# Max over neighbours by table lookup: groups of 7 columns become pairs of groups of 6

## The chip, the cores and the metric

The kernel runs on one core of one Trainium2 chip. A core has five engines with queues of their own, each in order: TensorE (PE, with its weight loads shown apart as PEld), VectorE (DVE), ScalarE (ACT), GpSimd (POOL) and SyncE (SP, which only issues transfers here). They meet through semaphores. TensorE writes to PSUM, 8 banks of 512 fp32 columns on 128 partitions; VectorE and ScalarE read it from there. The metric is the device time of one execution in microseconds, median over runs.

## The reference, cut to what matters

Four graph layers run over 16 graphs of 1024 nodes with 128 features, each followed by a residual addition and a layer norm: an attention (layer 0), an edge layer with a maximum (layer 1), a sum aggregation with a small MLP (layer 2), and three aggregations over a thinned adjacency (layer 3). The change is in layer 1:

```python
p = jnp.einsum('bnd,do->bno', x, W1 - W2)
q = jnp.einsum('bnd,do->bno', x, W2)
pre = p[:, :, None, :] + q[:, None, :, :] + b
h = jax.nn.relu(pre) * adj[..., None]
return jnp.max(h, axis=2)
```

As p[i] and b don't depend on the neighbour j, this is relu(p[i] + b + max of q[j] over the neighbours j of i), with zero for a node without neighbours.

Layer 3 thins the adjacency first ("dilation"), row by row in order: a row's removals take effect on later rows.

## The kernel before

**The maximum as a lookup.** The 1024 columns of a graph are cut into NG = 147 groups of GS = 7. For each group and feature, a table holds the maximum of q over each of the 128 subsets of the group (`tables_of`, L454 and L458: 7 doublings on VectorE for TG = 12 groups at a time). Which subset a node's neighbours form is found by one matmul: `lit` has +1 and −1 by the bits of the subset, and relu(count + 1 − size) is one at the right subset and zero elsewhere. That is `count`: a matmul `pm` (L688) and the ScalarE activation `hot` (L689), for each half of 512 nodes. The table is turned by a transpose (`table`, L700) so that subsets lie on partitions, and split into a high part in fp32r (L702, ScalarE) and the rest (`low_part`, L708, VectorE), for three groups at a time. `look_up` (L714) multiplies both parts with `hot` into `pg`, a PSUM tile of 128 features by 1024 nodes, of which there are two. VectorE then takes the running maximum `best` (L756).

**The slots.** `slot(s)` writes the instructions of one group, in the order in which each engine's queue gets them; there are 16 × 147 slots. It first lets other work advance, then writes for each half a count (of the group two slots ahead) and a lookup, then the table of a later group, then the maximum. The other work consists of generators ("streams") that yield what they need next with `ask`: engine, an estimated cost, whether they take or give back the one shared PSUM bank, what must have happened, a delay in slots. `advance` takes a step where the room of its engine (`ROOM`, refilled in every slot) allows. The streams are `scores` and `attend` (layer 0 of the next graph, with q and p of layer 1), `rest` (the end of layer 1 of the previous graph, and layer 2), and `tables_of`.

**The dilation** runs beside this, in 32 stripes of 32 rows. It yields how many slots later its next step comes. In a stripe, VectorE makes the counts (`low`, `rest`, L551 and L553), GpSimd goes through 31 rows (L566 to L576), the result `hit` goes to memory and back by SyncE's queue as `hit_p`, and VectorE goes on with `hit_T` (L587), ranks (L613, with ScalarE at L616) and `gone` (L619). GpSimd also issues, in its own queue, the loads of `E` (L482), `AT` (L647) and `An` (L638), and does the layer norms' rows. `An`, the adjacency of a graph, is read first by ScalarE's `off` (L313).

Where a graph's slots end, `rest` adds p to `best` (L380) and takes relu on ScalarE.

Of the kernel before, what the change touches and what calls it, by code (L numbers as in the profile page):

```python
# [42 lines left out]
GS = 7  # L43
CH = 126
GC = CH // GS
NG = -(-N // GS)
# [11 lines left out]
def subset_tables():  # L58

    s = np.arange(P)  # L60
    lit = np.zeros((CH, GC, P), np.float32)
    for j in range(CH):
        lit[j, j // GS] = np.where((s >> (j % GS)) & 1, 1.0, -1.0)
    size = sum((s >> k) & 1 for k in range(GS))
    return lit, (1.0 - size).astype(np.float32).reshape(P, 1)
# [3 lines left out]
def tile_graph_layers(ctx: ExitStack, tc, a, out):  # L69
# [30 lines left out]
    lit = consts.tile([CH, GC, P], F8, name="lit")  # L100
# [126 lines left out]
    def layers_012():  # L227
# [17 lines left out]
        def ask(engine, cost, take=False, give=False, same=False, delay=1, after=None, third=False, urgent=False):  # L245
            return engine, cost, take, give or urgent and None, 0 if same else delay, after, third
# [19 lines left out]
        def columns_of(dst, src, first=1):  # L266
            for h in range(2):
                yield ask("PE", 0.44, take=True, delay=1 if h else first)
                p = shared("ptr")
                for t in range(4):  # L270
                    nc.tensor.transpose(p[:, t * P:(t + 1) * P], src[:, 4 * h + t, :], ident)
                yield ask("A", 0.59, give=True, same=True)
                nc.scalar.copy(dst[:, halves[h]], p)

        def product_of(lhsT, rhs, dst, func, bias, delay=1):
            for h, s in enumerate(halves):
                yield ask("PE", 0.86, take=True, delay=1 if h else delay)
                p = shared("pp")
                nc.tensor.matmul(p, lhsT, rhs[:, s], start=True, stop=True)
                yield ask("A", 0.6, give=True, same=True)  # L280
                if bias is None:
                    nc.scalar.copy(dst[:, s], p)  # L282
                else:
                    nc.scalar.activation(dst[:, s], p, func, bias=bias)

        def scores(b):
# [51 lines left out]
            q = w4.tile([P, NG * GS], F32, name="q", bufs=2)  # L338
# [3 lines left out]
            happened["q", b] = now  # L342
            p = ps[b] = w4.tile([P, N], F32, name="p", bufs=2)
# [33 lines left out]
        def rest(b):  # L377
            best, p = bests.pop(b), ps.pop(b)
            yield ask("V", 1.2, after=("rest", b - 1) if b else None)
            nc.vector.tensor_add(best, best, p)  # L380
            yield ask("A", 1.06)
            nc.scalar.activation(best, best, AF.Relu)
            y = w4.tile([P, T, D], F32, name="y1", tag="y")
            for h in range(2):
                yield ask("PE", 0.44, take=True)
                pt = shared("ph")
                for t in range(4):
                    nc.tensor.transpose(pt[:, t * P:(t + 1) * P],
                                        best[:, (4 * h + t) * P:(4 * h + t + 1) * P], ident)
                yield ask("V", 0.66, give=True, same=True)  # L390
                nc.vector.tensor_add(y[:, 4 * h:4 * h + 4, :], X[b][:, 4 * h:4 * h + 4, :],
                                     pt.rearrange("p (t d) -> p t d", d=D))
            yield from norm(X[b], y)
# [49 lines left out]
        def tables_of(b):  # L443

            if b:
                yield ask("V", 0, urgent=True, after=("tables", b - 1))
            for g0 in range(0, NG, TG):
                n_g = min(TG, NG - g0)
                yield ask("V", 0.01, same=True, urgent=True, after=("q", b))
                made.append((b, g0))  # L450
                yield ask("V", 0.1, same=True, urgent=True, after=("used", *made[-3]) if len(made) > 2 else None)
                qg = qs[b].rearrange("o (g s) -> o g s", s=GS)
                sub = subs[b, g0] = w2.tile([P, TG, P], F32, name="sub", bufs=2)
                nc.vector.memset(sub[:, :n_g, 0:1], LOWEST)  # L454
                for k in range(GS):
                    n = 1 << k
                    yield ask("V", 0.06 + n * n_g / 960, same=(n < 8), urgent=True)
                    nc.vector.tensor_max(sub[:, :n_g, n:2 * n], sub[:, :n_g, 0:n],  # L458
                                         qg[:, g0:g0 + n_g, k:k + 1].to_broadcast([P, n_g, n]))
                happened["sub", b, g0] = now  # L460
            happened["tables", b] = now
# [10 lines left out]
        def dilation():  # L472
# [62 lines left out]
            for k in range(K):  # L535
# [21 lines left out]
                yield 1, 0.5  # L557
                gp = nc.gpsimd
                for n in range(R - 1):
# [17 lines left out]
                    yield 1.35, 0.06  # L577
# [7 lines left out]
                yield B * NG / K - 60.85, 0  # L585
# [6 lines left out]
                yield 1, 0.5  # L592
# [16 lines left out]
                yield 1, 0.5  # L609
                for q in range(Q):  # L610
                    rank = dil.tile([P, N], F32, name="rank", bufs=2)
                    for h, s in enumerate(halves):
                        nc.vector.tensor_tensor_scan(rank[:, s], E[:, q, s], E[:, q, s], rank[:, 511:512] if h else 0.0,  # L613
                                                     op0=ALU.add, op1=ALU.max)
                        yield 0.75, 1.2
                    nc.scalar.activation(rank, rank, AF.Abs, bias=centre[:, q:q + 1], scale=scale[:, q:q + 1])  # L616
                    yield 0.75, 0
# [4 lines left out]
                    yield 0.75, 1.3  # L622
# [5 lines left out]
                    yield 0.75, 0.8  # L628
# [26 lines left out]
        ROOM = {"PE": 0.6, "A": 0.6, "V": 1.4, "Pool": 9.0}  # L655
# [6 lines left out]
        def advance(engines):  # L662
            nonlocal bank_free
            for stream in list(streams):
                while True:
# [11 lines left out]
                    if give:  # L677
                        bank_free = now + 1
                    pending[stream] = [next(stream, None), now]

        def count(s, h):

            b, g = divmod(s, NG)
            c, r = divmod(g, GC)
# [6 lines left out]
        def table(s):  # L691

            b, g = divmod(s, NG)
            g0 = g - g % TG
            assert ("sub", b, g0) in happened, (s, [(x.__name__, pending[x]) for x in streams], room)
            pt = tables_bank("pt")[:, :3 * P]
            if g + 3 - g0 == min(TG, NG - g0):
                happened["used", b, g0] = now
            for k in range(3):
                nc.tensor.transpose(pt[:, k * P:(k + 1) * P], subs[b, g0][:, g - g0 + k, :], ident)  # L700
            high = w2.tile([P, 3 * P], F32R, name="high", bufs=2)
# [3 lines left out]
        def low_part(s):  # L705
            pt, high = tables[s]
            low = w2.tile([P, 3 * P], F32R, name="low", bufs=2)
# [3 lines left out]
        def look_up(s, h, pg):  # L711
            at = s % 3
            for k, part in enumerate(tables[s - at]):
                nc.tensor.matmul(pg[:, halves[h]], part[:, at * P:(at + 1) * P], hots[s][:, halves[h]],  # L714
                                 start=(k == 0), stop=(k == 1))

        def slot(s, last):

            nonlocal now, due
# [3 lines left out]
            b, g = divmod(s, NG)  # L723
            if s >= 0 and g == 0:
                bests[b] = w4.tile([P, N], F32, name="best", bufs=2)
# [7 lines left out]
            if s >= 0 and g % GC == 0:  # L733
                load_columns(b * (T + 1) + g // GC + 2)
            if (s + 1) % 3 == 0 and s + 1 < last:
# [4 lines left out]
            pg = psum.tile([P, N], F32, tag="wide", name="pg", bufs=2) if s >= 0 else None  # L740
            for h in range(2):
                if ahead is not None:
                    count(ahead, h)
                if s >= 0:
                    look_up(s, h, pg)
            if ahead is not None and ahead % 3 == 0:
                table(ahead)
            if s >= 0:
                while due <= s and s % 3 != 1:
                    after, cost = next(dilate, (B * NG, 0))  # L750
                    due += after
                    room["V"] -= cost
                if g == 0:
                    nc.vector.tensor_copy(bests[b], pg)
                else:
                    nc.vector.tensor_max(bests[b], bests[b], pg)  # L756
                hots.pop(s)

        dilate = dilation()
        due = 0.0  # L760
# [16 lines left out]
        with tc.manual_schedule(engines={mybir.EngineType.PE, mybir.EngineType.Activation, mybir.EngineType.DVE,  # L777
                                         mybir.EngineType.Pool}):
            planned = True
            for s in range(-2, B * NG):  # L780
                slot(s, B * NG)
# [313 lines left out]
```

## Time and profile before

| | us |
|---|---|
| runs: median of 3 (lowest to highest) | 7475.35 (7465.12 to 7479.03) |
| the profiled execution's own time | 7480.7 |
| its span in the profile | 7479.0 |
| busy: TensorE / weight loads | 6163.2 / 3818.6 |
| busy: VectorE | 5429.3 |
| busy: ScalarE | 4756.7 |
| busy: GpSimd | 3706.4 |
| `hot` L689, 4704 of 690 ns | 3119.1 |
| `best` L756, 2336 of 1214 ns | 2837.1 |

A group's line gives engine, operation, output and inputs with their shapes, the count, then busy time in us and the mean of one in ns, then how long the engine idled just ahead of these instructions and what ended most of that. Busy TensorE rows overlap each other: each reaches from its start to the modelled end of its last column, and the next starts before that. So a matmul's mean is its latency, not the pitch at which matmuls follow each other.

### The profile page before, as it was taken

The numbers are of one execution on the slowest core, as the hardware profiler recorded it, in microseconds if no ns is written. First come the engines' busy times: TensorE is split into PE (matmuls) and PEld (weight loads), VectorE is DVE, ScalarE is ACT, GpSimd is POOL, SyncE is SP. The second block draws the span as 40 slices with busy tenths as digits, with TensorE's granted clock in tenths as the row PEclk, the third lists the DMA queues.
The fourth block names the chain that finished last, engine by engine and source line by source line (L and its number), as shares of the span: only waits on it lengthen the run. The fifth ranks groups of instructions, "written<-read, shape, count | busy, mean of one in ns | idle before, by whom it ended". The sixth has DMA issues, their size and how long they took to land.

```text
span 7479.0 us, 89183 instructions
## 1 busy us (share of the span) xinstructions
PE 6163.2 (82%) x27882; PEld 3818.6 (51%) x27882; DVE 5429.3 (73%) x8907; ACT 4756.7 (64%) x7513; POOL 3706.4 (50%) x11637
## 2 busy tenths in 40 slices
PE   6878888888888878787978888787879767888996
PEld 4545555555554545454545455554545434555653
DVE  3878888878878878787878788787878764444453
ACT  4767777667776767676767676666667652333751
POOL 3455656565656555555555655555556531110116
PEclk8989999999999999999999999999989988888998
DMA  4121212121212121212121211111111025665544
GB/s 34 18 24 18 30 18 30 18 29 18 30 18 29 18 29 18 29 18 29 18 29 18 29 19 23 24 23 24 23 24 20 13 28 99 113 116 108 189 158 152
DMA packets 493633, 319.32 MB, mean 43 GB/s; under 512 B 315876, under 2 KB 444774, under 8 KB 489060
## 3 DMA queue, kind: packets, MB, share of 16 engines
q0 software_dynamic: 104880, 84.33, 13.0%
q1 hardware_dynamic: 383600, 228.10, 10.7%
q8 instruction: 219, 3.59, 0.2%
q10 hardware_dynamic: 4676, 1.19, 0.1%
q14 instruction: 258, 2.11, 0.1%
HBM read 414.24 MB, written 118.16 MB: 71 GB/s over the span
## 4 chain that ended last, share of the span: by engine, by line
PE 29%; DVE 15%; POOL 7%; ACT 5%; issue 3%; DMA 2%; ACTq 0%; SPq 0%; DVEq 0%; POOLq 0%
PE pg L714 9%; DVE best L756 6%; PE pagg L875 5%; PE pm L688 4%; DVE rank L613 2%; ACT hot L689 1%; DMA An<-in_adj_dram 1%; PE pa L411 1%; PE pav L368 1%; DVE sub L458 1%; PE psc L322 1%; PE pt L700 1%; PE po L889 1%; ACT rank L616 1%; DVE gone L619 1%
## 5 line engine op out<-in xcount | busy, mean ns | idle before, releaser
L689 ACT ACTIVATE hot<-pm,one_less 128x512 fp32r<-128x512 f32 x4704 | 3119.1, 690 | 1086.9 <-PE pm L688 1067.3
L756 DVE TENSOR_TENSOR best<-best,pg 128x1024 f32<-128x1024 f32 x2336 | 2837.1, 1214 | 776.7 <-PE pg L714 745.6
L714 PE MATMUL pg<-hot,high 128*128 128x512 f32 x4704 | 2825.2, 601 | 327.1 <-DVE best L756 324.8
L688 PE MATMUL pm<-AT,lit 126*128 126x512 fp8e4 x4704 | 1882.2, 400 | 165.6 <-ACT hot L689 163.8
L714 PE MATMUL pg<-hot,low 128*128 128x512 f32 x4704 | 1912.8, 407 | 0.0
L714 PEld LDWEIGHTS pg<-hot,high 128*128 128x128 f32 x4704 | 962.3, 205 | 772.5 <-DVE best L756 538.1
L688 PEld LDWEIGHTS <-lit 126*128 126x128 fp8e4 x4704 | 470.0, 100 | 1168.7 <-issue 1124.9
L714 PEld LDWEIGHTS pg<-hot,low 128*128 128x128 f32 x4704 | 935.2, 199 | 152.2 <-DVE low L708 21.0
L482 POOL DMA_DIRECT2D E<-in_adj_dram x128 | 70.3, 558 | 1621.3 <-DVE gone L619 1297.2
L458 DVE TENSOR_TENSOR sub<-sub,q 128x12 f32<-128x12 f32 (+7 forms) x1456 | 541.8, 372 | 32.7 <-ACT q L282 11.0
L566 POOL TENSOR_SCALAR sc<-low_counts,half_mask,rest 16x1 f32<-16x1 f32 x992 | 359.9, 363 | 252.5 <-DVE rest L553 156.1
L571 POOL TENSOR_SCALAR sc<-sc 16x1 f32<-16x1 f32 x992 | 412.9, 416 | 104.5
L708 DVE TENSOR_TENSOR low<-pt,high 128x384 fp32r<-128x384 f32 x784 | 431.6, 551 | 34.5 <-ACT high L702 34.3
L702 ACT CAST high<-pt 128x384 fp32r<-128x384 f32 x784 | 378.7, 483 | 102.4 <-PE pt L700 49.0
L700 PE MATMUL pt<-ident,sub 128*128 128x128 f32 x2352 | 406.2, 284 | 0.0
L568 POOL TENSOR_SCALAR sc<-sc 16x1 f32<-16x1 f32 x992 | 335.1, 338 | 107.1
L700 PEld LDWEIGHTS pt<-ident,sub 128*128 128x128 f32 x2352 | 322.6, 147 | 120.3 <-issue 14.3
L573 POOL TENSOR_SCALAR hit<-V,sc 16x31 bf16<-16x31 bf16 (+30 forms) x992 | 363.5, 366 | 0.0
L905 POOL TENSOR_TENSOR length<-length,mhalf 128x8 f32<-128x8 f32 x48 | 79.0, 1645 | 570.4 <-DVE length L904 570.4
L574 POOL TENSOR_SCALAR last_rank<-V,sc 16x31 f32<-16x31 bf16 (+30 forms) x992 | 356.4, 359 | 0.0
L322 PE MATMUL psc<-kT,qT 128*128 128x512 f32 x512 | 285.0, 640 | 67.2 <-DVE e L325 38.0
L862 ACT CAST m<-near 128x1024 fp32r<-128x1024 fp8e4 x256 | 253.8, 1044 | 119.3 <-PE pagg L875 54.2
(241 smaller groups left out, 9120.6 us busy)
## 6 DMA issues: line engine op xcount, KB each, us to landing
removed<-gone SPq DMA_DIRECT2D x128, 256.0 KB
An<-in_adj_dram POOLq DMA_DIRECT2D x16, 1024.0 KB, 13.5
E<-in_adj_dram POOLq DMA_DIRECT2D x128, 128.0 KB, 5.8
gone_all<-removed POOLq DMA_DIRECT2D x64, 256.0 KB, 12.4
near<-in_adjT_dram POOLq DMA_DIRECT2D x16, 1024.0 KB, 17.5
h<-x SPq DMA_DIRECT2D x32, 512.0 KB
kept<-near SPq DMA_DIRECT2D x16, 1024.0 KB
share<-share SPq DMA_DIRECT2D x32, 512.0 KB
```

Of the source, the lines that this page charges most:

```text
L458: nc.vector.tensor_max(sub[:, :n_g, n:2 * n], sub[:, :n_g, 0:n], qg[:, g0:g0 + n_g, k:k + 1].to_broadcast([P, n_g, n]))
L566: gp.tensor_scalar(half, mine, half_mask[:, m], rest[:, n:n + 1], op0=ALU.mult, op1=ALU.add)
L571: gp.tensor_scalar(to, at, sf, none, op0=ALU.subtract, op1=ALU.subtract)
L573: gp.tensor_scalar(hit[:, n, n + 1:], V[:, n, n + 1:], at, None, op0=ALU.is_equal)
L688: nc.tensor.matmul(pm, lit[:, r, :], AT[b * (T + 1) + c][:, halves[h]], start=True, stop=True)
L689: nc.scalar.activation(hots[s][:, halves[h]], pm, AF.Relu, bias=one_less)
L700: nc.tensor.transpose(pt[:, k * P:(k + 1) * P], subs[b, g0][:, g - g0 + k, :], ident)
L702: nc.scalar.copy(high, pt)
L708: nc.vector.tensor_sub(low, pt, high.bitcast(F32))
L714: nc.tensor.matmul(pg[:, halves[h]], part[:, at * P:(at + 1) * P], hots[s][:, halves[h]], start=(k == 0), stop=(k == 1))
L756: nc.vector.tensor_max(bests[b], bests[b], pg)
L875: nc.tensor.matmul(pa[:, s], piece[:, c, :], m[c][:, s], start=(c == 0 and k == 0), stop=(c == T - 1 and k == 1))
```

## The change

Columns are now taken in pairs of groups: PS = 12 columns, two groups of GS = 6, NP = 86 pairs in a graph, so 16 × 86 = 1376 slots. A group of 6 has 64 subsets, and the two groups of a pair share the 128 partitions: subsets of the first on 0 to 63, of the second on 64 to 127. One count matmul of 120 columns (ten pairs; before 126) serves both groups. `look_up` multiplies rows 0 to 63 into one bank and rows 64 to 127 into another, so `pg` is now 128 features by two groups by 512 nodes, one tile for each half of nodes. `best` has both groups apart, with a maximum for each half of nodes; `finish`, at a graph's end, takes the maximum over the two and adds p, which `rest` did before. Tables are turned and split for two pairs at a time. In the slot, both counts come first, then all lookups; TensorE's streams may advance once more behind the lookups, and those of the other engines between the two maxima, so delays are in half slots. The dilation's steps are spread anew over a stripe of 43 slots, and its step that needs the tables' bank is held to odd slots.

```diff
-GS = 7
-CH = 126
-GC = CH // GS
-NG = -(-N // GS)
+GS = 6
+PS = 2 * GS
+PC = 10
+CH = PC * PS
+NP = -(-N // PS)
...
-    lit = np.zeros((CH, GC, P), np.float32)
+    lit = np.zeros((CH, PC, P), np.float32)
     for j in range(CH):
-        lit[j, j // GS] = np.where((s >> (j % GS)) & 1, 1.0, -1.0)
+        a, k = divmod(j % PS, GS)
+        lit[j, j // PS, a * half:(a + 1) * half] = np.where((s >> k) & 1, 1.0, -1.0)
...
+            if b > 1:
+                yield ask("A", 0, same=True, after=("y1", b - 2))
             p = ps[b] = w4.tile([P, N], F32, name="p", bufs=2)
...
         def rest(b):
-            best, p = bests.pop(b), ps.pop(b)
-            yield ask("V", 1.2, after=("rest", b - 1) if b else None)
-            nc.vector.tensor_add(best, best, p)
-            yield ask("A", 1.06)
+            best = ps.pop(b)
+            yield ask("A", 1.06, after=("rest", b - 1) if b else None)
             nc.scalar.activation(best, best, AF.Relu)
...
-                sub = subs[b, g0] = w2.tile([P, TG, P], F32, name="sub", bufs=2)
+                subs[b, g0] = w2.tile([P, TG, P], F32, name="sub", bufs=2)
+                sub = subs[b, g0].rearrange("o t (a s) -> o (t a) s", a=2)
...
-                    yield 1.35, 0.06
+                    yield 0.95, 0.06, False
...
-                yield B * NG / K - 60.85, 0
+                yield B * NP / K - 37.75, 0, False
...
-                        yield 0.75, 1.2
+                        yield 0.34, 1.2, False
...
-        ROOM = {"PE": 0.6, "A": 0.6, "V": 1.4, "Pool": 9.0}
+        ROOM = {"PE": 1.2, "A": 0.8, "V": 1.4, "Pool": 9.0}
...
         def look_up(s, h, pg):
-            at = s % 3
+
+            at = s % 2
             for k, part in enumerate(tables[s - at]):
-                nc.tensor.matmul(pg[:, halves[h]], part[:, at * P:(at + 1) * P], hots[s][:, halves[h]],
-                                 start=(k == 0), stop=(k == 1))
+                for a in range(2):
+                    rows = slice(64 * a, 64 * a + 64)
+                    nc.tensor.matmul(pg[:, a], part[rows, at * P:(at + 1) * P], hots[s][rows, halves[h]],
+                                     start=(k == 0), stop=(k == 1))
+
+        def finish(b):
+
+            if b:
+                best = bests.pop(b - 1)
+                nc.vector.tensor_max(best[:, 0], best[:, 0], best[:, 1])
+                nc.vector.tensor_add(ps[b - 1], best[:, 0], ps[b - 1])
+            if b < B:
+                bests[b] = w4.tile([P, 2, N], F32, name="best")
...
-            pg = psum.tile([P, N], F32, tag="wide", name="pg", bufs=2) if s >= 0 else None
-            for h in range(2):
-                if ahead is not None:
+            if ahead is not None:
+                for h in range(2):
                     count(ahead, h)
-                if s >= 0:
-                    look_up(s, h, pg)
-            if ahead is not None and ahead % 3 == 0:
-                table(ahead)
+            pgs = []
             if s >= 0:
-                while due <= s and s % 3 != 1:
-                    after, cost = next(dilate, (B * NG, 0))
+                for h in range(2):
+                    pgs.append(psum.tile([P, 2, 512], F32, tag="wide", name="pg", bufs=2))
+                    look_up(s, h, pgs[h])
+                hots.pop(s)
+            now = s + 0.5
+            advance(("PE",))
+            if s >= 0:
+                while due <= s and (s % 2 or not wants_bank):
+                    after, cost, wants_bank = next(dilate, (B * NP, 0, False))
                     due += after
                     room["V"] -= cost
+            if ahead is not None and ahead % 2 == 0:
+                table(ahead)
+            for h, pg in enumerate(pgs):
+                if h:
+                    advance(("A", "V", "Pool"))
+                own = bests[b][:, :, halves[h]]
                 if g == 0:
-                    nc.vector.tensor_copy(bests[b], pg)
+                    nc.vector.tensor_copy(own, pg)
                 else:
-                    nc.vector.tensor_max(bests[b], bests[b], pg)
-                hots.pop(s)
+                    nc.vector.tensor_max(own, own, pg)
```

## The prediction

> **What bounds the kernel now.** I read the busy table by stretches first, then the groups by line, then who waited for whom, then the timeline. Three stretches: before the first maximum, the planned stretch of layers 0 to 2 (from the first `best` to the last, read off the groups and their first and last start), and layer 3. Columns: length, then each engine's busy time, clock, DMA share, GB/s.
>
> ```profile
> 0.00:141.50 141.50, 78.67 (x331) 51.23 (x332) 32.75 (x127) 45.86 (x71) 32.24 (x65) 0.86 0.64 44
> 141.50:6151.40 6009.90, 5013.30 (x22697) 3104.34 (x22695) 4816.35 (x7716) 4195.89 (x6808) 3412.51 (x11072) 0.94 0.17 23
> 6151.40:7479.00 1327.60, 1071.26 (x4856) 663.02 (x4856) 580.17 (x1067) 514.93 (x634) 261.70 (x500) 0.89 0.53 132
> ```
>
> Only the middle stretch is changed. It has 2352 slots (16 graphs of 147 groups), so a slot lasts 6009.9/2352 = 2.555 us. VectorE works 2.05 us of it, ScalarE 1.78, and no engine is full. Groups of the page (busy, mean ns, idle before):
>
> ```profile
> L689 ACT ACTIVATE hot<-pm,one_less 128x512 fp32r<-128x512 f32 x4704 | 3119.1, 690 | 1086.9 <-PE pm L688 1067.3
> L756 DVE TENSOR_TENSOR best<-best,pg 128x1024 f32<-128x1024 f32 x2336 | 2837.1, 1214 | 776.7 <-PE pg L714 745.6
> L714 PEld LDWEIGHTS pg<-hot,high 128*128 128x128 f32 x4704 | 962.3, 205 | 772.5 <-DVE best L756 538.1
> L458 DVE TENSOR_TENSOR sub<-sub,q 128x12 f32<-128x12 f32 (+7 forms) x1456 | 541.8, 372 | 32.7 <-ACT q L282 11.0
> L708 DVE TENSOR_TENSOR low<-pt,high 128x384 fp32r<-128x384 f32 x784 | 431.6, 551 | 34.5 <-ACT high L702 34.3
> ```
>
> TensorE's busy rows overlap each other, so I take its pitch from the timeline: one count, one high and one low lookup go from 2001.10 to 2001.78, 0.227 us each.
>
> ```profile
> 2001.10 0.38 PE L688 MATMUL pm<-AT,lit 126*128 126x512 fp8e4 x1
> 2001.12 0.58 PE L714 MATMUL pg<-hot,high 128*128 128x512 f32 x1
> 2001.55 0.40 PE L714 MATMUL pg<-hot,low 128*128 128x512 f32 x1
> 2001.78 0.39 PE L688 MATMUL pm<-AT,lit 126*128 126x512 fp8e4 x1
> ```
>
> A slot holds six of these (1.36 us), on average one table transpose (0.11) and 0.45 of other layers' matmuls: 1.92 us. VectorE and TensorE are thus nearly equal, and each waits for the other whenever their loads differ locally. VectorE's waits in the stretch (total us, times, longest):
>
> ```profile
> DVE best L756 <- PE pg L714: 745.6, 896, 30.6
> DVE e L325 <- PE psc L323: 166.4, 37, 27.7
> DVE hit_T L587 <- DMA hit_p<-hit: 69.5, 5, 33.3
> DVE gone L619 <- ACT rank L616: 62.7, 66, 2.9
> ```
>
> With L708 (31.8), L551 (25.7) and crumbs (91) that is 6009.9 − 4816.4 = 1193.5 us idle.
>
> **What the skill says.** "TensorE: Matmul & The Clock Gate", Part 3 (Packing small matmuls): matmuls whose rows lie in different row groups run at once; four of 32 rows measured 3.07 times faster. The trace of before has no such pair, so nothing here confirms it. Same page, LDWEIGHTS: a weight load costs by its columns, not its rows. The trace has 205 and 199 ns for 128 fp32r columns, against 0.227 us a matmul: hidden now, but halving the rows may not halve it. "TensorEngine Tiling (Array Packing)", Key Properties: changing the tiling mode drains TensorE; no price, none in the trace. Its Gotcha 1 wants the row tiles in different PSUM banks; `pg[:, 0]` and `pg[:, 1]` are. "VectorE: DVE Perf Modes", errata section: an fp32 tensor_tensor takes (N+151)/0.96 ns; 1224 for N = 1024, the trace has 1214.
>
> **VectorE's work.** Removed, in us: 2336 maxima at 1.214 and 16 copies at 1.211, 2856.5; the `sub` operations 541.8 and memsets 14.0 (208 at 67 ns); 784 `low` at 551 ns, 431.6; 16 additions of p at 1.221, 19.5. Sum 3863. Added: 2 × 1376 maxima and copies of the same 1024 elements, 3341. The halves are strided in `best` alone; I take no penalty. 688 `low` of 256 columns: 551 − 128/0.96 = 418 ns, 287. `sub`: 1456 operations over 16 × 147 × 127 elements at 0.96 per ns leave 158 ns fixed each; now 768 operations over 16 × 172 × 63 elements: 121 + 181 = 302. 128 memsets 9, 32 operations in `finish` 39. Sum 3978: 115 more. There are 448 fewer instructions, and neighbours on VectorE overlap by some 0.05 us in the records, so 22 of overlap goes too. VectorE is busy 4816 + 115 + 22 = 4953 us, 3.60 a slot of the new 1376.
>
> **ScalarE** loses 1952 `hot` at 690 ns (1347 us) and, in `high`, 379 becomes about 259 (0.84 ns a column between its 384 columns at 483 and a 512-wide copy at 590): 4196 falls to some 2730, 1.98 a slot. It no longer matters, and costs nothing while VectorE takes 3.6. **GpSimd** keeps every instruction. Its 31 rows and what is mixed in take 121 us from the counts of a stripe (L553) to the last L576, 124 to the issue of `hit_p`. The plan wants the result 35.2 slots after the counts, 137 us at 3.9 a slot: covered, uncovered below 3.52 a slot.
>
> **TensorE**, per new slot: two counts 0.45; eight lookups of 64 rows; one transpose 0.11; other layers 2352 × 0.45/1376 = 0.77. The lookups are the unknown. Pairs at once: 4 × 0.227 = 0.91. Weight loads one after the other: 8 × 0.2 = 1.6. No overlap at all: 1.82. The counts use 120 rows and the lookups 64, so the mode changes twice a slot; unseen, bounded by nothing and 0.3 us each (about one exposed weight load and a drain); I take 0.15. That gives 2.55, 3.2 or 3.4 us, all under VectorE's 3.60. I take pairs at once: separate row halves and separate banks are just what the page asks for.
>
> **What VectorE still waits for.** I laid out the order of instructions of both kernels slot by slot with these prices. Before, TensorE has more to do than VectorE in 1269 of 2352 slots, by 602 us in all; 746 were lost, a factor 1.24. After, 264 of 1376 slots, 124 us: 154 lost. The `e` wait of 166 has another cause. GpSimd issues the load of `An` in its own queue, and ScalarE's `off` (L313) waits for it to land, 13.5 us later. Behind `off` stand the `hot` activations, then the lookups and maxima. A stripe's plan sums to 72.5 slots where half a graph has 73.5, so stripes run ahead and `An` stands behind row 1 of its stripe in graph 2, row 10 in graph 8, row 21 in graph 15. ScalarE's wait grows accordingly: 8.2, 12.1, 16.4 up to 29.2 us. In the new order a stripe sums to 43 = 86/2, `An` is always ahead of row 0, and `off` stands six slots (23 us) into the stripe: about 20 us left. `hit_T` 40. `gone`: 32 stand directly behind their scan and wait a ScalarE pass of 1.24 us and more, 65. `low` 28, counts 26, crumbs 91 × 1376/2352 = 53. Together 386.
>
> **Sum.** Stretch 4953 + 386 = 5339, 671 less than 6010. Span 7479 − 671 = 6808; the profiled execution's own time 7480.7 becomes 6810; it lies 5 over the median shown (7475), so I forecast 6805 us. Set-up and layer 3 are untouched and keep their 1469 us.
>
> **Rivals.** (1) Weight loads pass one at a time: lookups 1.6 us a slot. For: 0.2 us a load whatever the rows, and they are as long as a matmul. Against: they go to different rows. TensorE's surplus is then 335 us in 421 slots, times 1.24 = 415: 261 more, 7065 us. (2) The change doesn't do what it says: eight lookups in a row, surplus 495, times 1.24 = 614: 460 more, 7265. Still faster, since the counts have fallen from 4704 to 2752. (3) Slower: the mode change, between the counts (L693) and the lookups (L722) and back. Break-even is 6010/1376 = 4.37 us a slot. Before, a slot was 0.5 longer than its fuller engine, so TensorE has to reach 3.87. With lookups in a row it has 0.45 + 1.82 + 0.11 + 0.77 = 3.15; two changes must cost 0.72, 0.36 us each. At 0.5 us each TensorE has 4.15, a slot 4.65, the stretch 6400: 7865 us. Against: that is more than a weight load and a matmul together. (4) VectorE nearly full, the surplus lost in the two buffers of `pg`: idle 200, 6620 us.
>
> **How the numbers follow.** Pairs at once 0.50 (own range 6680 to 6950), weight loads 0.24, in a row 0.13, VectorE nearly full 0.05, slower 0.06, no change 0.02. All but the last two are faster by more than 0.2%, about what a measurement of this kernel can tell from no change: 0.92. The range 6640 to 7260 holds all of the forecast's, nearly all of the weight loads' and half of the third.
>
> **What would show it.** `best` maxima 2752 at about 1.21 us and VectorE over 90% busy in the stretch; its wait for `pg` near 150 us instead of 746; ScalarE's wait for `An` gone; `hot` at 2752. Pairs at once: four lookups of a half in about 0.45 us; loads in a row: 0.8; in a row: 0.9. A mode change is a gap between the last count and the first lookup that no wait explains. A slower maximum on the strided halves, or a lower granted clock on a less busy TensorE (0.94 now), would break the sum.

## The result, and the profile after

| | before | after |
|---|---|---|
| median of 4 runs (lowest to highest), us | 7474.06 (7465.12 to 7479.03) | 7494.59 (7489.59 to 7515.01) |
| ratio, 95% interval | | 1.0034 [1.0013, 1.0055] |
| profiled execution, own time / span | 7480.7 / 7479.0 | 7493.2 / 7491.3 |
| stretch of layers 0 to 2 | 6009.9 | 6027.0 |
| VectorE busy / idle in it | 4816.4 / 1193.5 | 4876.5 / 1150.5 |

The forecast was 6805 us. The changed kernel takes 0.3% longer than the one before. The busy table by stretches (length, then PE, PEld, DVE, ACT, POOL busy, clock, DMA share, GB/s) of the kernel after:

```profile
0.00:141.00 141.00, 80.77 (x338) 51.35 (x342) 36.30 (x126) 47.47 (x75) 31.91 (x65) 0.87 0.65 43
141.00:6168.00 6027.00, 4480.30 (x21236) 2193.65 (x21356) 4876.51 (x7267) 2781.14 (x4757) 3288.28 (x11066) 0.83 0.16 22
6168.00:7491.00 1323.00, 1066.15 (x4856) 660.07 (x4856) 580.57 (x1067) 514.56 (x634) 265.09 (x506) 0.89 0.55 135
```

VectorE does what the sum said (4953 forecast, 4877 measured), ScalarE too (2730 and 2781), and TensorE has 533 us less of busy rows. The groups by line show each step of VectorE's account in its place, 1211 ns for the maxima on strided halves and 416 for `low` (418 forecast):

```profile
L782 DVE TENSOR_TENSOR best<-best,pg 128x1024 f32<-128x1024 f32 x2720 | 3207.4, 1211 | 704.6 <-PE pg L722 701.5
L694 ACT ACTIVATE hot<-pm,one_less 128x512 fp32r<-128x512 f32 x2752 | 1739.2, 686 | 1059.5 <-PE pm L693 1056.4
L722 PEld LDWEIGHTS pg<-hot,high 64*128 64x128 f32 x5504 | 583.5, 208 | 2068.7 <-DVE best L782 1595.5
L463 DVE TENSOR_TENSOR sub<-sub,q 128x24 f32<-128x24 f32 (+11 forms) x768 | 301.8, 394 | 24.3 <-ACT q L285 11.0
L713 DVE TENSOR_TENSOR low<-pt,high 128x256 fp32r<-128x256 f32 x688 | 286.0, 416 | 36.0 <-ACT high L707 33.7
```

What did not come is the fall of VectorE's idle time: 386 us forecast, 1150 measured, where the kernel before had 1193. Its waits in the stretch (total us, times, longest):

```profile
DVE best L782 <- PE pg L722: 701.5, 340, 18.0
DVE hit_T L592 <- DMA hit_p<-hit: 129.7, 16, 23.5
DVE gone L624 <- ACT rank L621: 77.9, 46, 3.5
DVE low_counts L556 <- PE pc L553: 56.3, 30, 3.6
```

The wait for `pg` keeps most of its total and changes its kind: 896 waits of 0.8 us in the mean before, 340 of 2.1 us now. ScalarE's growing wait for `An` is gone from the stretch, as forecast.

**Pairs do run at once.** The timeline of TensorE in one slot; "x2" at the lookups are the two row halves, and their starts in the trace lie 0.003 us apart, those of their weight loads 0.003 to 0.004:

```profile
3212.50 0.60 PE L693 MATMUL pm<-AT,lit 120*128 120x512 fp8e4 x2
3213.03 0.50 PE L722 MATMUL pg<-hot,high 64*128 64x512 f32 x2
3213.37 0.40 PE L722 MATMUL pg<-hot,low 64*128 64x512 f32 x2
3213.60 0.39 PE L722 MATMUL pg<-hot,high 64*128 64x512 f32 x2
3213.83 0.40 PE L722 MATMUL pg<-hot,low 64*128 64x512 f32 x2
3214.16 0.70 PE L325 MATMUL psc<-kT,qT 128*128 128x512 f32 x1
```

Eight lookups take some 1.0 us (0.34 for the first pair, then 0.23 for each of three). From the start of the last count (3212.72 in the trace) to the first lookup it is 0.31 us where count follows count at 0.22, and from the last pair to the next matmul of 128 rows 0.32 where pairs follow each other at 0.23. So a change between matmuls of different numbers of rows (the prediction's mode change) costs some 0.09 us each way; the first pair's longer 0.34 may belong to it too. So rivals 1 (loads one at a time), 2 (lookups in a row) and 3 (a dear mode change) fall by this trace alone. TensorE is fast enough, and VectorE waits for it all the same.

**Where the waits stand.** Two kinds carry the wait for `pg`. Once in a graph, in slot 64 of 86, TensorE stands at the transposes `ptr` of layer 0's result and waits for GpSimd to finish its layer norm X; 195 of the 701 us lie behind that. TensorE's own waits:

```profile
PE ptr L274 <- POOL X L222: 164.7, 16, 15.7
PE pe L363 <- ACT e L335: 68.8, 43, 1.6
PE pav L373 <- ACT eT L366: 50.2, 58, 1.3
PE pe L363 <- ACT eT L366: 43.4, 49, 1.3
```

The other 500 us are waits of mostly under 4 us, some 400 of them in the same dozen slots of every graph. TensorE's last three lines belong to the attention: its transposes `pe` wait for ScalarE's exponential `e` and for the copy `eT`, its products `pav` for `eT`. Before, `pe` already waited for `e`; the waits for `eT` are new:

```profile
PE pe L358 <- ACT e L332: 47.9, 75, 4.0
PE pe L358 <- ACT eT L361: 6.5, 6, 1.9
PE pav L368 <- ACT eT L361: 3.8, 4, 1.3
```

One of the waits, from the timelines of VectorE, ScalarE and TensorE (start, duration):

```profile
3217.41 2.34 DVE L782 TENSOR_TENSOR best<-best,pg 128x1024 f32<-128x1024 f32 x2
3218.66 0.37 ACT L707 CAST high<-pt 128x256 fp32r<-128x256 f32 x1 [1.64 <-PE pt L705]
3218.92 1.15 ACT L335 ACTIVATE e<-e,top 128x1024 f32<-128x1024 f32 x1
3220.22 0.66 PE L363 MATMUL pe<-ident,e 128*128 128x128 f32 x4 [1.60 <-ACT e L335]
3221.24 0.50 PE L722 MATMUL pg<-hot,high 64*128 64x512 f32 x2
3222.01 1.22 DVE L782 TENSOR_TENSOR best<-best,pg 128x1024 f32<-128x1024 f32 x1 [1.93 <-PE pg L722]
```

The attention's `pe` comes half a slot behind the exponential `e` that it reads. In TensorE's queue the next counts and lookups stand behind `pe`. `e` is late (ahead of it in ScalarE's queue stood `high`, which waited 1.64 us for TensorE's transposes `pt`), TensorE idles 1.60 us, and then VectorE 1.93.

### The profile page after: what moved, and what is told of

Read it like the earlier page. It is cut to its first block, busy times and chain, and to the rows that moved or that the text cites. A ratio compares the mean times of both kernels' runs of the same rounds, so it can differ in the third digit from the quotient of the medians.

```text
span 7491.3 us, 84114 instructions
## 1 busy us (share of the span) xinstructions
PE 5627.2 (75%) x26430; PEld 2905.1 (39%) x26554; DVE 5493.4 (73%) x8459; ACT 3343.2 (45%) x5465; POOL 3585.3 (48%) x11637
## 4 chain that ended last, share of the span: by engine, by line
DVE 30%; PE 29%; POOL 22%; issue 8%; ACT 6%; DMA 4%; SPq 0%; another core or an unknown queue 0%; DVEq 0%; ACTq 0%; POOLq 0%
DVE best L782 13%; PE pg L722 7%; PE pagg L901 5%; DVE rank L618 3%; PE pav L373 3%; POOL sc L576 2%; PE pm L693 2%; DVE sub L463 2%; POOL hit L578 2%; DVE gone L624 2%; POOL sc L571 2%; POOL last_rank L579 2%; POOL sc L573 2%; PE pe L363 2%; PE psc L325 2%
## 5 line engine op out<-in xcount | busy, mean ns | idle before, releaser
L782 DVE TENSOR_TENSOR best<-best,pg 128x1024 f32<-128x1024 f32 x2720 | 3207.4, 1211 | 704.6 <-PE pg L722 701.5
L694 ACT ACTIVATE hot<-pm,one_less 128x512 fp32r<-128x512 f32 x2752 | 1739.2, 686 | 1059.5 <-PE pm L693 1056.4
L722 PE MATMUL pg<-hot,high 64*128 64x512 f32 x5504 | 1485.8, 536 | 911.6 <-DVE best L782 888.4
L722 PEld LDWEIGHTS pg<-hot,high 64*128 64x128 f32 x5504 | 583.5, 208 | 2068.7 <-DVE best L782 1595.5
L722 PE MATMUL pg<-hot,low 64*128 64x512 f32 x5504 | 1229.0, 442 | 0.0
L693 PE MATMUL pm<-AT,lit 120*128 120x512 fp8e4 x2752 | 955.9, 431 | 13.2 <-ACT hot L694 6.0
L722 PEld LDWEIGHTS pg<-hot,low 64*128 64x128 f32 x5504 | 612.1, 218 | 30.8
L693 PEld LDWEIGHTS <-lit 120*128 120x128 fp8e4 x2752 | 271.1, 107 | 323.8 <-issue 260.3
L373 PE MATMUL pav<-v,eT 128*128 128x128 f32 x2048 | 330.7, 317 | 52.4 <-ACT eT L366 52.3
L373 PEld LDWEIGHTS pav<-v,eT 128*128 128x128 f32 x2048 | 290.5, 222 | 124.7 <-ACT eT L366 75.9
```

Of the source, the lines that this page charges most:

```text
L373: nc.tensor.matmul(pav, eT[:, c, :], values[b][:, c, :], start=(c == 0), stop=(c == T - 1))
L693: nc.tensor.matmul(pm, lit[:, r, :], AT[b * (T + 1) + c][:, halves[h]], start=True, stop=True)
L694: nc.scalar.activation(hots[s][:, halves[h]], pm, AF.Relu, bias=one_less)
L722: nc.tensor.matmul(pg[:, a], part[rows, at * P:(at + 1) * P], hots[s][rows, halves[h]], start=(k == 0), stop=(k == 1))
L782: nc.vector.tensor_max(own, own, pg)
```

## The experiments

All medians are of 4 runs (5 for the kernel without the `low` lookups); the ratio, with its 95% interval, is to the kernel before, run on the same chip beside it, where it took 7463.1 to 7474.1 us. Differences between runs are differences of these medians; as the kernel before itself differs by 11 us between these measurements, differences of that size say nothing.

**1. Is it the clock or TensorE's pace?** The granted clock fell from 0.927 to 0.844, and 18% of the lookups with `high` run slowly (0.79 us instead of 0.50). Three runs changed TensorE's instructions alone.

Each count issued twice, to keep TensorE busier:

```diff
-            nc.tensor.matmul(pm, lit[:, r, :], AT[b * (T + 1) + c][:, halves[h]], start=True, stop=True)
+            for _ in range(2):
+                nc.tensor.matmul(pm, lit[:, r, :], AT[b * (T + 1) + c][:, halves[h]], start=True, stop=True)
```

> The changed kernel with every count matmul issued twice into the same bank, so TensorE has 2752 more matmuls of 0.22 us (605 us) just ahead of the lookups, where it waits for VectorE anyway. Nothing else changes. Clock theory (the granted clock fell from 0.93 to 0.84 as TensorE idles, and the slow matmuls cost the expected gain): the clock rises to 0.90 or more and the time falls by 100 us or more. Queue-order theory (the waits come from steps of other streams that stand ahead of the lookups, at full clock too): the clock rises, the pg wait does not fall, and the time lies between 7490 and 7650 us. Pace theory (TensorE has too much to do for VectorE): the time rises by 200 us or more.

Measured: 7578.5 us, 1.0150 [1.0135, 1.0165]; clock 0.893. The clock rises and nothing is won; VectorE waits 799 us for `pg`, where the changed kernel waits 701. Read the other way: 2752 more counts at 0.22 us, 605 us of TensorE's time, cost 84 us.

The `low` lookups left out:

```diff
-            for k, part in enumerate(tables[s - at]):
+            for k, part in enumerate(tables[s - at][:1]):
...
-                                     start=(k == 0), stop=(k == 1))
+                                     start=True, stop=True)
```

> The changed kernel without the lookups' second part: the matmuls with low are left out (the operation that makes low stays), so the maxima are of the rounded tables. TensorE loses 5504 of 11008 lookups, about 0.46 us a slot, 630 us in all; VectorE keeps all its work. Pace theory (TensorE's lookups of 64 rows are what VectorE waits for): the pg wait falls from 701 to under 450 us and the time by 250 us or more. Queue-order theory: the pg wait falls by no more than 150 us and the time by 50 to 150 us. Clock theory: the clock falls below 0.84 and eats part of it, the time changes by less than 100 us.

Measured: 7437.3 us, 0.9957 [0.9942, 0.9971]; VectorE waits 643 us for `pg` instead of 701. Half of all lookups, 2752 pairs of 0.23 us or 633 us, are worth 57 us. Pace falls as a cause. So does the clock as the main one: at 0.777 the kernel is faster than at 0.844, though no run moved the clock alone.

High and low of the first row half, then of the second, meant to put the halves one after the other:

```diff
-            for k, part in enumerate(tables[s - at]):
-                for a in range(2):
+            for a in range(2):
+                for k, part in enumerate(tables[s - at]):
```

> The changed kernel, with the four lookups of a half in another order: high and low of rows 0 to 63, then high and low of rows 64 to 127. Two neighbours now use the same rows, so only the middle two can run at once: three times 0.23 us instead of two, 0.46 us a slot more, 630 us in all. Pace theory (running pairs at once is what the kernel lives on): the time rises by 200 us or more above 7494. Queue-order theory: TensorE had the time to spare, the pg wait rises by less than 150 us, the time by 0 to 120 us. If the two row halves never ran at once in the first place: no change.

Measured: 7503.4 us, 1.0049 [1.0034, 1.0064]. The edit did not do what it was meant to. The timeline of this kernel shows the halves still in pairs, high with high, though in the kernel's text the first half's low stands between them; all 2752 groups of four do the same:

```profile
3211.78 0.50 PE L722 MATMUL pg<-hot,high 64*128 64x512 f32 x2
3212.11 0.40 PE L722 MATMUL pg<-hot,low 64*128 64x512 f32 x2
```

So it tests nothing of the price of lookups in a row. It shows that the order between row halves in the trace is not the one in which the kernel writes them; whether the chip or a step of the program's translation put them so, no run tells.

**2. Is it what stands ahead of the lookups?** First GpSimd's norm alone: the readers of X asked for four slots later.

```diff
-            happened["X1", b] = now
+            happened["X1", b] = now + 4
```

> The changed kernel, but layer 1's stream of the next graph starts four slots later after the layer norm of the attention has been handed to GpSimd. In the changed kernel TensorE waits once a graph, at slot 64, some 13 us for that norm's rows (164.7 us in 16 waits), and VectorE's wait for pg has 195 us of its 701 behind it. Queue-order theory: those waits all but vanish, the pg wait falls from 701 to about 520 us, and the time from 7494 to about 7330 us. Rival, GpSimd is short of time as such: the wait turns up elsewhere (hit_T, now 130 us, or the next norm), and the time stays within 40 us of 7494. Rival, the clock: [...]the granted clock would rise from 0.84 by some hundredths at most.

Measured: 7492.8 us, 1.0039 [1.0024, 1.0054]: nothing. VectorE's two waits show why (after: 701.5 and 129.7):

```profile
DVE best L782 <- PE pg L722: 556.6, 354, 5.8
DVE hit_T L592 <- DMA hit_p<-hit: 210.3, 16, 25.9
```

145 us went from the lookups, 81 came at `hit_T`, which waits for the same GpSimd, and 59 at `low` (31.4 to 90.0), whose cause no run took apart. For the larger part, a wait for a late engine was moved to its next reader.

Then the half-slot delay of the attention alone, `pe` and `pav` half a slot further behind their sources:

```diff
-                happened["e", b, t] = now
+                happened["e", b, t] = now + 0.5
...
-                    yield ask("PE", 0.9, take=(h == 0))
+                    yield ask("PE", 0.9, take=(h == 0), delay=1)
```

> The changed kernel, but two of the attention's TensorE steps stand half a slot later in the plan: the transposes of e, which wait for ScalarE's exponential, and the products with v, which wait for ScalarE's copy of eT. Each of the two now has at least one more pair of lookups ahead of it. Queue-order theory: TensorE's waits pe<-e (68.8 us) and pav<-eT (50.2) vanish, the pg wait falls from 701 to about 500 us, the time from 7494 to about 7350 us. Pace theory and clock theory: the same work at the same clock, the pg wait stays within 60 us of 701 and the time within 40 us of 7494.

Measured: 7314.3 us, 0.9797 [0.9783, 0.9812]; 180 us less than the changed kernel, by two delays. VectorE still waits 608.8 us for `pg`, where some 500 were expected, for TensorE's wait for X rose from 165 to 217. What of VectorE's wait lies behind X rose from 195 to 278 us, while `hit_T` fell from 130 to 34, so GpSimd costs about the same in sum. The rest of the wait for `pg` fell from 506 to 330 us, about the gain.

Both edits:

> The two edits of before together: the two attention steps half a slot later, and layer 1's stream four slots after the attention's norm. With the first alone TensorE still waits 226.7 us for GpSimd's norm (17 times, in slot 64), but VectorE's wait for hit_T is down to 33.9. Queue-order theory: the waits add up, the norm's wait falls under 80 us and the time from 7314 to about 7150 us. GpSimd theory (its rows and norms fill the second stripe of a graph, so a wait taken away at slot 64 comes back as hit_T at slot 78): hit_T rises by 80 us or more, the time stays above 7250 us.

Measured: 7334.6 us, 0.9820 [0.9805, 0.9834]. `pg` 465, but `hit_T` 204: the waits do not add up, as the expectation's second theory had it. A third edit gave that step more time, by spreading the removal's steps closer behind it:

```diff
-                yield B * NP / K - 37.75, 0, False
+                yield B * NP / K - 36.25, 0, False
...
-                        yield 0.34, 1.2, False
+                        yield 0.265, 1.2, False
```

(and 0.265 in its three other steps)

> The same, and in every stripe the dilation's result hit_T is asked for 1.5 slots later (36.7 slots after the counts, before 35.2), with the rank steps packed closer behind it (0.265 slots apart, before 0.34). GpSimd theory: each of the 32 stripes gives GpSimd some 4 us more, hit_T's wait is under 60 us, and the time is 50 to 100 us below that with the two edits alone. Rival: the denser ranks cost as much as they give (gone waits for rank, more uneven slots), within 30 us of it.

Measured: 7377.7 us, 0.9881 [0.9864, 0.9897]. `hit_T` fell to 124, `gone` rose from 42 to 154 and `pg` to 499: a loss.

All half-slot delays whole again, with the rooms raised so that the streams still end in time:

```diff
-        def ask(engine, cost, take=False, give=False, same=False, delay=0.5, after=None, third=False, urgent=False):
+        def ask(engine, cost, take=False, give=False, same=False, delay=1, after=None, third=False, urgent=False):
...
-        ROOM = {"PE": 1.2, "A": 0.8, "V": 1.4, "Pool": 9.0}
+        ROOM = {"PE": 1.6, "A": 1.2, "V": 1.8, "Pool": 9.0}
...
-                        bank_free = now + 0.5
+                        bank_free = now + 1
```

(also 1 for 0.5 in `columns_of` and `product_of`)

> The changed kernel with the streams' delays of half a slot set to a whole slot, as the kernel before has them, and the rooms raised (TensorE 1.6, ScalarE 1.2, VectorE 1.8) so that the streams are still done in time. Queue-order theory: a step that needs another engine's result then always has a slot's lookups in between, TensorE's waits for e, eT, psc's bank (69, 93 and 48 us) fall by more than half, the pg wait falls by 150 us or more, and the time by 100 us or more. Rival: the rooms let steps bunch up, so local surpluses grow by as much, and the time stays within 50 us of 7494.

Measured: 7158.8 us, 0.9581 [0.9566, 0.9595]: 336 less than the changed kernel. It leaves nothing out and is faster than both kernels. TensorE's waits of the attention are all but gone, while that for X has grown:

```profile
PE ptr L274 <- POOL X L222: 280.0, 15, 22.1
PE pe L363 <- ACT e L335: 1.6, 1, 1.6
```

The rooms alone:

> The control to that: the changed kernel with the raised rooms alone (TensorE 1.6, ScalarE 1.2, VectorE 1.8), delays at half a slot. Queue-order theory: more steps per slot and the same short distances, so no better than 7494 us, 0 to 80 us above. Rival, the rooms are what matters: it is as fast as the run with whole-slot delays.

Measured: 7724.8 us, 1.0338 [1.0323, 1.0353]. More room with half-slot delays makes it worse by 230 us, so the gain is not the rooms'. Whole delays with the old rooms were not run.

**3. Is it GpSimd?** Two of the ten GpSimd operations of a row (the expectation says eleven) were left out, `last_rank` and its addition to `hit` (one rule of which neighbours are removed). These kernels compute another result in layer 3, which reads the thinned adjacency ("layer 2" in some expectations), and serve for measuring alone:

```diff
-                    last = small.tile([B, R], F32, name="last_rank")
...
-                    gp.tensor_scalar(last[:, n + 1:], V[:, n, n + 1:], to, None, op0=ALU.is_le)
-                    gp.tensor_add(hit[:, n, n + 1:], hit[:, n, n + 1:], last[:, n + 1:])
```

They are 347 and 216 ns, with 83 ns idle ahead of the second: 0.65 us a row, 20 us a stripe of 31 rows, 641 us of GpSimd's time in all. In the changed kernel:

> The changed kernel with two of the eleven GpSimd operations of a dilation row left out: last_rank is not computed and not added to hit, so rows lose their removals of the last rank and layer 3 sees another thinned adjacency. 347 and about 230 ns and their gaps times 31 rows: some 19 us less GpSimd work in each of 32 stripes; every other engine has the same instructions. GpSimd theory (its rows and norms are late, and the plan makes TensorE and VectorE wait for them in their queues): TensorE's wait for the norm (164.7 us) falls under 40, VectorE's for hit_T (129.7) under 20, the pg wait from 701 to about 520 us, and the time from 7494 to about 7200 us. Rival, only the steps' order among TensorE, ScalarE and VectorE counts: the time falls by less than 60 us.

Measured: 7248.7 us, 0.9701 [0.9686, 0.9715], 246 less. TensorE's wait for X falls from 165 to 38 us and the one at `hit_T` from 130 to 2: 254 us, about the gain. With both later readers of experiment 2:

> The same two GpSimd operations left out of the kernel with both streams' steps later (7334.6 us, hit_T 204 us, norm 81 us). GpSimd theory: what the later steps at slot 64 gave was given back at hit_T; without GpSimd's lateness it stays, hit_T under 30 us, and the time about 7080 us. Rival: the wait moves on to a third place, and the time stays above 7200 us.

Measured: 7057.5 us, 0.9445 [0.9428, 0.9462], 277 below its pair. With whole delays:

> The kernel whose half-slot delays are all whole ones again (7158.8 us, VectorE idle 818 us in the stretch of layers 0 to 2), with two of the dilation's GpSimd operations for each of the 31 earlier nodes of a stripe left out (the comparison with the last rank and the addition to hit), so that other nodes are removed and layer 2's values differ; the numbers of instructions on the other engines stay. Theory (what is left over the forecast is GpSimd's lateness): TensorE's wait for X, 289 us, falls to some 40, hit_T's 63 goes, and VectorE's idle time falls to 400-520: 6750-6870 us for the kernel, close to the forecast of 6805. Rival (it is given back elsewhere, as when one place alone was moved): less than 60 us come, 7100-7160.

Measured: 6838.2 us, 0.9153 [0.9139, 0.9167]. VectorE's largest waits in the stretch:

```profile
DVE best L779 <- PE pg L719: 190.3, 257, 5.2
DVE gone L621 <- ACT rank L618: 79.9, 46, 3.6
DVE e L328 <- PE psc L326: 44.8, 53, 1.1
```

A slot is 5373.3/1376 = 3.91 us, and `pg` costs 190 us. The mechanism of the forecast is there, once two things stand out of its way. That 6838 lies so near to 6805 is partly luck: VectorE's work is 83 us under the forecast and its idle time 117 over it, in a kernel that leaves work out.

The chain of work that ended last (shares by engine) tells the same from one line of the page. The kernel after:

```profile
DVE 30%; PE 29%; POOL 22%; issue 8%; ACT 6%; DMA 4%; SPq 0%; another core or an unknown queue 0%; DVEq 0%; ACTq 0%; POOLq 0%
```

with whole delays:

```profile
POOL 37%; DVE 26%; PE 20%; issue 11%; ACT 3%; DMA 3%; SPq 0%; DVEq 0%; POOLq 0%; ACTq 0%
```

and with whole delays and the two operations left out:

```profile
DVE 43%; PE 35%; issue 8%; POOL 7%; ACT 5%; DMA 2%; DVEq 0%; another core or an unknown queue 0%; POOLq 0%; SPq 0%; ACTq 0%
```

GpSimd is busy for little over half of the stretch in the kernel after, and yet it is a fifth of the chain, over a third once TensorE's order is mended, and falls back to 7% when its rows are shorter.

The traces show the two causes apart. Each graph's 86 slots hold two stripes of the removal, one in each half. Mean length of a half, from the starts of `best`:

| us | first half | second half |
|---|---|---|
| after | 192.9 | 184.2 |
| X's readers later | 192.3 | 184.3 |
| attention half a slot later | 180.5 | 185.5 |
| whole delays | 173.3 | 182.4 |
| after, two operations a row left out | 192.6 | 168.9 |
| whole delays, two operations a row left out | 171.5 | 164.5 |

The delays move the first half alone, and GpSimd's shorter rows almost only the second, where TensorE waits for X. The forecast's stretch comes to 5339/32 = 167 us for each half. The doubled counts, the missing lookups and the raised rooms leave the second half at 184 us too.

**4. What limits the kernel before?** The same two operations left out there:

> The kernel before, with the same two GpSimd operations of the dilation left out (layer 2's values differ). Theory: GpSimd limits the kernel before less, because its slots were 5.1 us long in the mean and its dilation is spread over longer slots, and the wait for An (170 us on ScalarE) stands: 7380-7460 us, 20 to 90 below. Rival (GpSimd limits it as much): 200-250 us below, 7215-7270.

Measured: 7200.0 us, 0.9638 [0.9622, 0.9654]: 269 less, so the theory (20 to 90) missed and its rival held: GpSimd costs the kernel before as much. There it shows at `An` too, whose load stands in GpSimd's queue: ScalarE's wait for it falls from 176 to 79 us, VectorE's for `e` from 189 to 88. The expectation also had a slot of before twice too long; it is 2.56 us, and the plan gives a row 1.35 × 2.56 = 3.45 us, where 31 rows took some 117 us from the first to the last, 3.9 each.

The drift of `An` taken out of the kernel before, by one number:

```diff
-                yield B * NG / K - 60.85, 0
+                yield B * NG / K - 59.85, 0
```

> The kernel before, with one number changed: a stripe of the dilation is planned as 73.5 slots (half a graph) where it was 72.5, so An keeps its place ahead of the stripe's rows in GpSimd's queue. The prediction counted some 145 us for this. If that is right, ScalarE's wait for An (170.2 us) falls under 30 us and the time from 7463 to about 7310 us. Rival: GpSimd is no earlier with its rows, so the wait turns up behind the norms or at hit_T, and the time stays within 50 us of 7463.

Measured: 7281.0 us, 0.9753 [0.9738, 0.9767]: 187 less, the wait for `An` gone (one of 4.5 us is left of 176), at the price of `hit_T` (69 to 149). The number also puts the step at `hit_T` one slot later, and TensorE's wait for X fell with it (126 to 28 us in the whole run), so the 187 us are not the wait for `An` alone. Both:

> The kernel before with the dilation's pause one slot longer (7281.0 us alone: no wait for An, hit_T waits 149 us), and the same two GpSimd operations left out (layer 2's values differ). Theory (GpSimd is behind the hit_T wait and little else): hit_T's 149 us go, TensorE's wait for X is 23 as it was: 7110-7190 us. Rival (given back to the lookups): over 7220.

Measured: 7143.4 us, 0.9561 [0.9547, 0.9576]: 138 below b_nodrift; `hit_T` 149 to 8.

Medians side by side, all without the wait for `An`:

| us | before without the drift | after | after with whole delays |
|---|---|---|---|
| all of GpSimd's work | 7281.0 | 7494.6 | 7158.8 |
| two operations a row left out | 7143.4 | 7248.7 | 6838.2 |

Down the columns GpSimd's 641 us cost 138, 246 and 321. From the second column to the third the half-slot delays and their rooms cost 336 and 410. From the first to the third, pairs with whole delays gain 122 with GpSimd as it is and 305 without its excess.

## Why the prediction was wrong

Point by point, in the stretch of layers 0 to 2:

| us | forecast | after | whole delays | whole, less GpSimd |
|---|---|---|---|---|
| VectorE busy | 4953 | 4876.5 | 4874.2 | 4870.1 |
| its wait for `pg` | 154 | 701.5 | 448.4 | 190.3 |
| `An` | 20 | 0 | 0 | 0 |
| `hit_T` | 40 | 129.7 | 63.2 | 6.2 |
| `gone` | 65 | 77.9 | 79.3 | 79.9 |
| `low` | 28 | 31.4 | 2.8 | 3.5 |
| counts | 26 | 56.3 | 27.3 | 25.8 |
| others | 53 | 153.7 | 196.8 | 197.5 |
| idle | 386 | 1150.5 | 817.8 | 503.2 |

**VectorE's and ScalarE's work: right**, VectorE's 76 us too high, 1.6%. No penalty for the strided halves, `sub` and `low` as reckoned.

**TensorE: right in kind.** Pairs at once; 1.03 us for eight lookups where 0.91 were taken, the mode change 0.09 where 0.15; with both changes 1.21 us, the sum that was taken. By these prices TensorE's work in a slot stays well under VectorE's 3.60.

**The step that failed is "What VectorE still waits for": surplus times 1.24.** Of the 764 us of idle time that the forecast lacks, 547 are the wait for `pg` (154 against 701), 90 `hit_T`, and 101 the crumbs ("others"). The step compared the work of TensorE and VectorE slot by slot and scaled by what was lost before. But the doubled counts and the halved lookups moved the time by 14% and 9% of the matmul time that they added or removed. The wait for `pg` consists for the most part of TensorE standing, in order, at another stream's instruction whose input is not there. An estimate from the trace gives each wait of VectorE to TensorE's longest wait in the 4.5 us ahead of it: of 702 us, some 195 go to `ptr`, nearly all behind GpSimd, 285 to layer 0's `pe` and `pav`, half a slot behind ScalarE, 150 to the projections `pp` and `pv`, and only 39 have no such wait ahead. Before, 377 of 746 us had none, and 156 went to `ptr`: the factor 1.24 had such waits inside it as if they were surplus. The change shortened the distances from one slot to half a slot, as "The change" says, and the prediction did not price that. A distance of 2.56 us became half of 4.38, 2.19, and `e` needs a ScalarE pass of 1.15 and whatever stands ahead of that in its queue.

**"GpSimd keeps every instruction, covered": wrong.** It checked one reader of GpSimd, `hit_p`, at the mean pace of a slot. GpSimd has a second one: the norms stand in the same queue between the rows, and TensorE waits for them. TensorE's wait stands in each graph's second stripe (slot 64 of 86, with whole delays slot 76); in the kernel with whole delays that half-graph lasts 182 us in the mean, without the two operations 164. Of the 321 us between those two, 287 lie there (16 × 17.9).

**`An`: right**, and its cause shown: one number in the plan takes the wait away in the kernel before. That number is worth 187 us there, more than the 145 that the forecast gave to `An`, and it does not belong to the pairs. Against the kernel before with that number mended, the change as a whole is 214 us slower.

**The rivals** 1 to 3 put a price on TensorE's array, 4 on the buffers; none was about the order in TensorE's queue or about GpSimd. The time came out on the slower side, without rival 3's mechanism.

**What stays open:** in the kernel with whole delays and light rows 503 us of idle are left against 386. Its "others" hold 76 us of `e` and 33 of `hT`, waits for layer 0's and layer 2's own matmuls; no run took them apart. How the 336 us split between delays and rooms stays open too, and why GpSimd's lateness binds almost only the second half of a graph.

## What to carry to other kernels

A wait for a matmul is not a shortage of matmul time: look at what stands just ahead of it in TensorE's queue, and what that waits for; a run that adds or removes matmuls told the two apart here. When a schedule counts in slots and the slot changes its length, price each distance again in microseconds against its producer's latency. And take an engine with low busy share seriously where its results have two readers: here, moving one reader later handed most of the wait to the other, and the chain that ended last showed it.

## What the runs showed of the hardware

- Two matmuls on row halves 0 to 63 and 64 to 127, in separate banks, start 0.003 us apart (median of 5504 pairs), and so do their fp32r weight loads of 0.19 us. Pairs follow each other at 0.23 us, the second 0.34 behind the first.
- In the trace the two halves keep their own order, but not the kernel's between them: with high, low of the first half written ahead of high, low of the second, both highs started together (0.007 us apart), before both lows.
- A change from 120-row to 64-row matmuls took 0.31 us from start to start, and one from 64 rows to 128 took 0.32, against 0.22 and 0.23 without a change: some 0.09 us more.
- The granted clock was lower with less matmul work: 0.927 before, 0.893 with the counts doubled, 0.844 after, 0.777 with half the lookups. The kernel at 0.777 was faster than the one at 0.844, so the clock is not the main thing that the change lost its gain to; no run moved the clock alone.
